# Four-layer graph attention stack: the third layer's PSUM banks emptied by one ScalarE copy with the relu, reciprocal and scaling done in SBUF

## Chip, cores and metric

One core of one Trainium2 chip runs the whole program. The metric is the device time of one execution in microseconds. A run before the change took 2668.16 us (median of 3 runs, 2663.21 to 2668.47).

## What is computed

16 graphs of 1024 nodes with 256 features pass through four attention layers, each with a layer norm and a relu ahead of it and a residual behind it. The first three layers have four heads of 64 features, the fourth has one head of 256. The third layer, which the change touches, is (cut to what matters; in this stack `adj` holds 0 and 1 only):

```python
h = relu(layernorm(x)); h = einsum('bnd,hde->bhne', h, W)
weight = leaky_relu(e_src[..., :, None] + e_dst[..., None, :], 0.01)
attention = softmax(where(adj == 0, -1e9, weight), axis=-1)
dst = einsum('bhij,bhje->bhie', attention, h) + bias
out = relu(dst) + h
out = (out - mean(out)) / sqrt(var(out) + 1e-6) * gamma + beta    # over each head's 64 features
x = x + out
```

## The kernel before, in words

**One head.** The nodes are cut in 8 blocks of 128. For a head, VectorE makes 8 tiles `p` of 128x1024: the numerators of the softmax from one block of nodes to all 1024. `cover` makes one in a single instruction out of a row `r` (128x1024, in PSUM), a factor `fac` for each node of the block and the mask. There are 12 buffers for `p` (`p0` to `p11`). TensorE then multiplies each tile with the block's values `vals`, which carry one more column, so that column 64 of the product is the softmax's denominator. `gather` does that for one half of the 1024 nodes: 8 matmuls, and 8 tiles add up in one PSUM bank `po` of 128 x 4 x 65. The two halves of a head are two groups with a bank each, the second some tiles behind the first. There are two such banks (`ps_o`, `bufs=2`), so a new group can start only when the group before the last one has been emptied.

**Emptying a bank.** `evacuate` runs once for each group. In the first two layers (`u.shared`) ScalarE copies the whole bank, 128x260, into an SBUF tile `att` (three buffers, `ATTS`). In the third layer the bias is already added to the values (`v_flat`), and the bank is emptied in this order: VectorE takes the reciprocal of the four denominators out of PSUM into `inv`; then ScalarE reads each of the four 128x64 blocks out of PSUM, scales it by its reciprocal, applies the relu and writes it to `att`. After both halves `finish` adds `h` on GpSimd (`att <- att,v`), takes statistics on VectorE (`st <- att`), normalizes on ScalarE (`att <- att,s`), and adds to `x_cur` on GpSimd.

**What else ScalarE does.** It copies the rows `r` from SBUF to PSUM (`spread_row`, 128x1024), each up to 3 tiles before the head that uses it; it turns the relu and copies of the projections out of PSUM (`hT`, `v`); it checks the masks (`seen`), scales the fourth layer's results (`y`).

**The order of the work.** The order on every engine is fixed when the program is built: a planner (`Plan`) keeps an estimated free time for each engine and steps through jobs, which are generators; each `yield` names the engine of the next step and when it may go. Of the steps that could start next on an engine, it takes the one that is due first. The wrappers `act`, `dve`, `pe`, `pool` and `sp` issue an instruction and book its estimated cost with `plan.spend`; a call through `nc.scalar` or `nc.vector` issues it without booking it. On the chip each engine runs its list in order and waits with semaphores. Since most instructions are recorded by the wrapper, the profile gives nearly all of them line 515; they are told apart by their tiles. The graphs and layers are interleaved by the table `ORDER`, so that the work of two or three layers of different graphs is in flight at a time.

The lines that the text needs: the banks `ps_o` (617), `cover` (1218), `gather` (1278), `evacuate` (1312), `finish` (1341).

Of the kernel before, what the change touches and what calls it, by code (L numbers as in the profile page):

```python
# [16 lines left out]
AF = mybir.ActivationFunctionType  # L17
# [519 lines left out]
def fast_path(  # L537
# [21 lines left out]
    nc = tc.nc  # L559
    ctx.enter_context(tc.manual_schedule())  # L560
    plan = Plan()
    pe, act, dve, pool, sp = (
        plan.engine(e, name)
        for e, name in (
            (nc.tensor, "PE"),
            (nc.scalar, "ACT"),
            (nc.vector, "DVE"),
            (nc.gpsimd, "POOL"),
            (nc.sync, "SP"),
        )  # L570
# [5 lines left out]
    QUAD = 4  # L576
# [701 lines left out]
    def gather():  # L1278

        u, i, h, j, p, slot, _ = covered.pop(reach()[1])  # L1280
        w = u.w
        if (u, i, h) not in groups:
            groups[u, i, h] = [sums_bank(w + 1), 0, len(opened)]
            opened.append(None)
        g = groups[u, i, h]
        po = g[0]
        at = h * (w + 2)
        for q in range(QUAD):


            for c in range(0, P, P // 2):
                pe.matmul(
                    po[c : c + P // 2, q, :],
                    p[:, q * P + c : q * P + c + P // 2],
                    u.vals[:, j, at : at + w + 1],
                    start=(g[1] == 0 and q == 0),
                    stop=(g[1] == NB - 1),
                    skip_group_check=True,
                )
        leave(slot)  # L1300
        g[1] += 1
        if g[1] == NB:
            u.gathered, u.last = u.gathered + 1, plan.now
            u.v_done = u.v_done or u.shared and u.gathered == 2 * H
            add(-(10**6), evacuate(u, i, h, po, g[2]), plan.now)
# [6 lines left out]
    def evacuate(u: "Unit", i: int, h: int, po, turn: int):  # L1312

        w = u.w
        q = slice(i * QUAD, (i + 1) * QUAD)
        yield "ACT" if u.shared else "DVE", lambda: finishing[0] < ATTS or (u, h) in taking
        if (u, h) not in taking:
            finishing[0] += 1
            taking[u, h] = [work.tile([P, NB, w + 1], F32, name="att", bufs=ATTS), 0]
        att = taking[u, h][0]  # L1320
        if u.shared:
            act.copy(att[:, q, :], po)
        else:
            inv = u.inv[:, h, q]
            dve.reciprocal(inv, po[:, :, w])
            yield "ACT", None
            for k in range(QUAD):
                act.activation(att[:, i * QUAD + k, :w], po[:, k, :w], AF.Relu, scale=inv[:, k : k + 1])
        opened[turn] = plan.now
        taking[u, h][1] += 1  # L1330
        if taking[u, h][1] == 2:

            by = -(10**6) if u.layer < 2 or at_tile[0] > len(tiles) - LAST else at_tile[0] + LATER
            add(by, finish(u, h, att[:, :, :w], att[:, :, w]), plan.now)
# [249 lines left out]
    def add(until, gen, ready, first=None):  # L1584
        jobs.append([until, ready, *(first or next(gen))[:2], gen])
# [103 lines left out]
```

## Time and profile before

| | |
|---|---|
| runs | 2663.21, 2668.16, 2668.47 us |
| profiled execution | 2667.53 us, span 2665.8 us, granted clock 0.997 |
| PE busy, weight loads (PEld) | 2578.2 us, 2207.9 us |
| VectorE (DVE) | 2342.0 us, 3723 instructions |
| ScalarE (ACT) | 1272.3 us, 3378 instructions |
| GpSimd (POOL) | 1890.4 us |
| DMA | 184.44 MB, mean 69 GB/s |

The span is the time from the first instruction to the last. A group's row in the profile names line, engine, operation, `out<-in` by tile, the shape and the number of instructions; behind the bar stand the busy time in us and the mean of one in ns, and behind the second bar the idle time of that engine just ahead of the group's instructions and what ended it. A row of the order of time gives start, length, engine, the group and, in brackets, the idle time before it and its releaser. An idle time "by issue" is one that no other instruction ended.

### The profile page before, as it was taken

The page shows a single profiled execution, that of the slowest core. Times are in us where ns is not written, and L with a number is a line of the kernel's source. Part 1 is how long each engine was busy: PE and PEld are TensorE (multiplying, and loading weights), DVE is VectorE, ACT ScalarE, POOL GpSimd, SP SyncE. Part 2 cuts the span into 40 slices and gives each one's busy share as a digit, 9 for nine tenths or more (in the row PEclk, how much of TensorE's full clock was granted, in tenths as well). Part 3 has the DMA queues.
Part 4 walks back from the last instruction along what each step waited for, and adds up shares of the span by engine and source line. Part 5 has one row for each costly group of instructions (what it writes and reads, how often), then busy time and mean ns, then how long its engine had stood idle before and what let it go on. Part 6 is the DMA issues. An engine that isn't in the chain of part 4 may idle for free. (4 is left out here: it accounts for less than half of the span.)

```text
span 2665.8 us, 132436 instructions
## 1 busy us (share of the span) xinstructions
PE 2578.2 (97%) x59354; PEld 2207.9 (83%) x59354; DVE 2342.0 (88%) x3723; ACT 1272.3 (48%) x3378; POOL 1890.4 (71%) x3375
## 2 busy tenths in 40 slices
PE   9999999999999999999999999999999999899998
PEld 7888887787988788889888788988778798888775
DVE  6799998897999797889998897999888699998984
ACT  4633563654346456533564644356364553443441
POOL 5556888765778877747887875688787565977761
PEclk9999999999999999999999999999999999999999
DMA  8533233443132253313314441323334441111100
GB/s 133 84 75 73 59 69 69 76 87 71 64 66 63 63 85 82 76 57 77 72 55 82 88 72 59 83 50 75 74 74 79 83 85 57 53 47 55 40 23 32
DMA packets 211122, 184.44 MB, mean 69 GB/s; under 512 B 150640, under 2 KB 184560, under 8 KB 210544
## 3 DMA queue, kind: packets, MB, share of 16 engines
q1 hardware_dynamic: 143088, 159.10, 20.7%
q0 software_dynamic: 67456, 16.78, 10.3%
q8 instruction: 467, 7.65, 1.2%
q14 instruction: 111, 0.91, 0.1%
HBM read 191.77 MB, written 34.39 MB: 85 GB/s over the span
## 5 line engine op out<-in xcount | busy, mean ns | idle before, releaser
L515 DVE SCALAR_TENSOR_TENSOR p<-r,fac,mask 128x1024 f32<-128x1024 f32 (+2 forms) x2032 | 2075.7, 1079 | 159.8 <-PE pp L515 80.8
L515 PE MATMUL po<-v,p 128*64 128x65 f32 x32992 | 1060.9, 224 | 36.4 <-issue 15.8
L515 PEld LDWEIGHTS po<-v,p 128*64 128x64 f32 x32992 | 1021.5, 138 | 87.9 <-issue 30.8
L515 PEld LDWEIGHTS po<-v_flat,p 128*64 128x64 f32 x16384 | 507.8, 138 | 56.8 <-issue 24.4
L515 PE MATMUL po<-v_flat,p 128*64 128x65 f32 x16384 | 525.0, 223 | 29.4 <-issue 14.7
L515 PE MATMUL pp<-wa,hT 128*64 128x264 f32 (+1 forms) x4032 | 474.2, 385 | 0.1
L515 PE MATMUL pp<-v_one,p 128*64 128x257 f32 x3584 | 403.6, 380 | 3.2 <-ACT y L515 2.9
L515 PEld LDWEIGHTS pp<-wa,hT 128*64 128x64 f32 x4032 | 278.4, 137 | 132.1 <-ACT v L515 0.4
L515 PEld LDWEIGHTS pp<-v_one,p 128*64 128x64 f32 x3584 | 248.6, 136 | 128.0 <-ACT y L515 4.6
L515 POOL TENSOR_SCALAR hn<-x_cur,rs 128x256 f32<-128x256 f32 x504 | 274.6, 558 | 33.3 <-PE pp L515 29.3
L515 POOL TENSOR_TENSOR att<-att,inv 128x512 f32<-128x512 f32 x128 | 133.7, 1045 | 221.2 <-DVE inv L515 207.7
L515 ACT COPY att<-po 128x260 f32<-128x260 f32 x256 | 96.2, 376 | 377.1 <-PE po L515 353.1
L515 ACT COPY v<-pp 128x264 f32<-128x264 f32 (+1 forms) x392 | 148.5, 379 | 215.0 <-PE pp L515 213.8
L515 POOL TENSOR_TENSOR x_cur<-att,x_cur 128x512 f32<-128x512 f32 x190 | 225.8, 1188 | 14.9
L515 ACT COPY r<-rows 128x1024 f32<-128x1024 f32 x190 | 194.0, 1021 | 21.8 <-DVE p L515 15.5
L515 ACT ACTIVATE att<-att,s 128x64 f32<-128x64 f32 x512 | 190.9, 439 | 23.3 <-POOL s L515 23.0
L515 ACT ACTIVATE hT<-pp 128x512 f32<-128x512 f32 x250 | 136.4, 598 | 128.1 <-PE pp L515 127.4
L515 ACT ACTIVATE att<-po,inv 128x64 f32<-128x64 f32 x512 | 118.7, 321 | 145.6 <-DVE inv L515 143.6
L515 POOL TENSOR_TENSOR y<-y,x_cur 128x256 f32<-128x256 f32 x116 | 84.3, 732 | 131.6 <-ACT y L515 112.1
L515 POOL TENSOR_TENSOR v<-v,fac 128x512 f32<-128x512 f32 x131 | 136.2, 1064 | 11.5 <-ACT fac L515 11.4
L515 DVE BATCH_NORM_STATS2 st<-x_cur 128x6 f32<-128x256 f32 x400 | 138.3, 411 | 3.3 <-DMA x_cur<-in_x_dram 2.9
L515 PE MATMUL pp<-ident,hn 128*128 128x128 f32 x1000 | 137.0, 280 | 0.2 <-DVE row L515 0.2
(124 smaller groups left out, 2150.0 us busy)
## 6 DMA issues: line engine op xcount, KB each, us to landing
rows<-line SPq DMA_DIRECT2D x190, 512.0 KB
out_dram<-y SPq DMA_DIRECT2D x128, 128.0 KB
x_cur<-in_x_dram SPq DMA_DIRECT2D x112, 128.0 KB
near<-in_adj_dram POOLq DMA_DIRECT2D x112, 128.0 KB, 4.3
rows_one<-line SPq DMA_DIRECT2D x13, 512.0 KB
x_cur<-in_x_dram SPq DMA_DIRECT2D x4, 512.0 KB
line<-row SPq DMA_DIRECT2D x96, 8.0 KB
block<-in_adj_dram POOLq DMA_DIRECT2D x4, 256.0 KB, 10.4
```

Of the source, the lines that this page charges most:

```text
L515: r = call(*a, **k)
```

## The change

In the third layer's branch of `evacuate` the bank is emptied by one ScalarE instruction, which applies the relu and copies all four blocks with their denominators (128x260) to `att`. VectorE takes the reciprocals from `att` in SBUF, and ScalarE scales the four 128x64 blocks in place in `att`. The denominators are positive, and so are the factors, so that relu and scaling may change places. The copy is not booked in the plan; the reciprocal and the scalings are booked with the costs that they had.

```diff
         if u.shared:
             act.copy(att[:, q, :], po)
         else:
             inv = u.inv[:, h, q]
-            dve.reciprocal(inv, po[:, :, w])
+            nc.scalar.activation(att[:, q, :], po, AF.Relu)
+            nc.vector.reciprocal(inv, att[:, q, w])
+            plan.spend("DVE", *plan.cost("DVE", "reciprocal", (inv,), {}))
             yield "ACT", None
             for k in range(QUAD):
-                act.activation(att[:, i * QUAD + k, :w], po[:, k, :w], AF.Relu, scale=inv[:, k : k + 1])
+                one, of = att[:, i * QUAD + k, :w], inv[:, k : k + 1]
+                nc.scalar.activation(one, one, AF.Copy, scale=of)
+                plan.spend("ACT", *plan.cost("ACT", "activation", (one, of), {}), [], [att.tensor.name])
```

## Prediction

> **What bounds the kernel now.** I read the page's first part, then the busy time of each engine by stretch, then the weight loads and the order of time inside one stretch, and last the groups by form. The page alone points at TensorE:
>
> ```profile
> PE 2578.2 (97%) x59354; PEld 2207.9 (83%) x59354; DVE 2342.0 (88%) x3723; ACT 1272.3 (48%) x3378; POOL 1890.4 (71%) x3375
> ```
>
> The table by stretch says otherwise for a part of the run. Its columns are the stretch, its length, then busy time and count for PE, PEld, DVE, ACT and POOL.
>
> ```profile
> 758.40:829.90 71.50, 67.42 (x1944) 62.19 (x1940) 71.33 (x109) 40.35 (x124) 60.45 (x106) 1.00 0.26 55
> 1246.30:1317.60 71.30, 66.99 (x1947) 62.02 (x1941) 71.26 (x108) 40.23 (x124) 61.27 (x108) 1.00 0.26 55
> 1731.70:1802.90 71.20, 66.59 (x1919) 61.36 (x1915) 71.20 (x110) 40.28 (x124) 61.31 (x108) 1.00 0.27 55
> 2261.50:2332.80 71.30, 63.91 (x1790) 59.41 (x1786) 71.03 (x122) 32.40 (x93) 63.70 (x111) 0.98 0.17 55
> 829.90:1246.30 416.40, 408.81 (x9151) 346.26 (x9151) 362.68 (x578) 201.60 (x524) 299.22 (x536) 1.00 0.34 74
> ```
>
> The run repeats every 488 us. In each period there is a stretch of 71 us in which VectorE is busy for 71.3 of 71.5 us; the same holds for 270 to 342 us (71.75 of 72.00). In the other 416 us VectorE has 54 us of idle time and TensorE is the bound. That PE reads 94% inside a stretch is its pipelining; the weight loads at the end of one stretch show who leads:
>
> ```profile
> 822.83 1.01 PEld L515 LDWEIGHTS po<-v,p 128*64 128x64 f32 x32 [0.18 <-DVE p L515]
> 824.02 1.01 PEld L515 LDWEIGHTS po<-v,p 128*64 128x64 f32 x32 [0.18 <-DVE p L515]
> 825.21 1.01 PEld L515 LDWEIGHTS po<-v,p 128*64 128x64 f32 x32 [0.18 <-DVE p L515]
> 826.40 1.01 PEld L515 LDWEIGHTS po<-v,p 128*64 128x64 f32 x32 [0.18 <-DVE p L515]
> ```
>
> Every tile is waited for: 1.19 us from tile to tile, VectorE's own pace, while 1.01 us of loading would do. So a microsecond put into VectorE there lengthens the run, and a microsecond taken from TensorE earlier in the stretch is only waited out later in it.
>
> [...] By the 97% the sum below would be rival A; by the weight loads (87% in the stretch, VectorE 99.8%) it is the forecast.
>
> **The change, part by part.** 16 graphs x 4 heads x 2 halves make 128 evacuations. The built programs hold the same instructions in the same order on PE, DVE, POOL and SP, so no DMA moves. Only ScalarE gets 128 more instructions, each where the planner chose the reciprocal. The rows:
>
> ```profile
> L515 ACT COPY att<-po 128x260 f32<-128x260 f32 x256 | 96.2, 376 | 377.1 <-PE po L515 353.1 <-POOL hn L515 11.3 <-POOL x_cur L515 9.9
> L515 ACT ACTIVATE att<-po,inv 128x64 f32<-128x64 f32 x512 | 118.7, 321 | 145.6 <-DVE inv L515 143.6 <-DVE wide L515 0.8
> L515 DVE RECIPROCAL inv<-po 128x4 f32<-128x4 f32 x128 | 22.5, 176 | 21.4 <-PE po L515 20.3
> L515 PE MATMUL po<-v_flat,p 128*64 128x65 f32 x16384 | 525.0, 223 | 29.4 <-issue 14.7 <-ACT att L515 10.8 <-DVE p L515 1.5
> ```
>
> 1. *The added copy.* The same shape without the relu takes 0.376 us; at 128x512 the relu (598 ns) is 12 ns over the copy (586 ns). So 0.38 us, and 128 x 0.38 = 49 us of ScalarE, which is idle for 52% of the span. Off the path by itself; its price is in whom it delays.
>
> 2. *The bank.* Before, it was held from the group's end through the reciprocal and four scalings (0.93 us): 1.2 us at least and 1.65 us in the middle one of the 128. Now about 0.43 us. TensorE waited 10.8 us for it. All of these waits but one (0.26 us) lie in or beside the five stretches, for instance:
>
> ```profile
> 768.10 0.33 DVE L515 RECIPROCAL inv<-po 128x4 f32<-128x4 f32 x2
> 768.37 1.75 ACT L515 ACTIVATE att<-po,inv 128x64 f32<-128x64 f32 x8 [6.40 <-DVE inv L515]
> 769.35 1.85 PE L515 MATMUL po<-v_flat,p 128*64 128x65 f32 x56 [1.15 <-ACT att L515]
> ```
>
> With the bank free earlier TensorE starts earlier and is then late for nothing but VectorE's tiles, as it already was by 771.9. Worth about 0 where VectorE leads; 10.8 us is the other end.
>
> 3. *The reciprocal's new wait.* It now stands behind the copy: group end + 0.05 + 0.38 + 0.03 us, or later if ScalarE is busy. Behind it on VectorE stand all later covers (1.19 us each), for which TensorE waits. The stretch at 758, from the records of each instruction (group ends are the last matmul's):
>
> | evacuation | group ends | VectorE came | new copy ends | wait added |
> |---|---|---|---|---|
> | 1 | 758.28 | 758.37 | 758.71 | 0.37 |
> | 2 | 760.15 | 760.83 | 760.97 | 0 |
> | 3, 4 | 767.73, 768.20 | 768.10, 768.24 | 768.16, 768.63 | 0.42 for both |
> | 5 | 781.80 | 782.44 | 782.23 | 0 |
> | 6 | 782.27 | 783.70 | 784.5 | 0.8 |
> | 7 | 794.30 | 794.63 | 795.1 | 0.45 |
> | 8 | 796.28 | 797.16 | 797.6 | 0.45 |
>
> Row 2 is covered by the shift of row 1. In row 6 the copy queues behind the four scalings of row 5, and these behind a row copy (1.02 us) that row 5's copy holds up. In rows 7 and 8 it queues behind work that ScalarE has already begun (a row copy until 794.78; scalings until 797.27). Sum 2.5 us. Read the same way, the stretches at 270, 1246, 1732 and 2261 give 2.2, 2.5, 2.1 and 1.6 us. Together 10.9 us, all on the path, since VectorE has no idle time left there to absorb it.
>
> 4. *The other 88 evacuations* (and their waits, 0 to 1.4 us each, some 39 us by the same reckoning) fall where tiles lie 0.7 to 20 us ahead of TensorE and VectorE still idles, mostly for TensorE. Covered: 0. Without that cover: 39 us.
>
> 5. *Scalings from SBUF.* No row shows one with a single scalar operand. Bounds: 0.23 us each as now, from PSUM; 0.345 us as the normalization's `att<-att,s` (SBUF, two scalar operands; eight in 2.76 us). I take the first, the nearer in operands; the other adds 0.45 us to four scalings, which reaches VectorE only in row 6: at most 2 us in all. The reciprocal's source: 176 ns from PSUM, 196 ns for 128x8 from SBUF: nothing. [...]
>
> 6. *What is held up behind the copy.* On ScalarE: four row copies (at 265, 752, 1241 and 1727 us) that now wait 4 to 6 us for a group's end; the cover that first reads such a row stands behind four other covers and two sets of statistics, 5 us and more after the new copy's end, so 0. The `hT` and `v` copies come at most 0.15 us late by the same reckoning: 0 to 1 us. The copy also takes its `att` buffer sooner than the scalings did, from POOL; the scalings never waited for POOL in the trace, so 0.
>
> 7. *The end.* The last graph's third layer feeds its fourth, and TensorE idles at 2587 (2.8 us) and 2607 us (1.8 us) for that chain. One evacuation is 0.4 us longer, two if both halves count: 0.8 us.
>
> Sum: 10.9 + 0.8 = about +12 us. The profiled execution took 2667.53 us (span 2665.8), by 0.6 us the median of the runs shown (2668.16). I forecast **2679 us**. Faster or slower by 0.2% is 5.3 us, about what can be told from no change.
>
> **Rivals.**
>
> A. *TensorE is the bound throughout* (page: 97%) and the bank waits come off: 2667.5 - 10.8 = 2657 us. It decides if VectorE's lead in the stretches is regained before the next one, that is if the waits in step 3 find idle time. Against it: 0.2 us of idle time in 71.5. Chance 0.12.
>
> B. *Hidden.* The gain of step 2 pays for step 3, or the copies find ScalarE earlier than I queue them (rows 6 to 8 fall away): 2664 to 2672, say 2669. For it: TensorE runs several us behind VectorE in the middle of each stretch. Chance 0.2.
>
> C. *More than queued.* Waits add up since each shifts the next group's end, and part of step 4's 39 us or the slower scalings reach the path: 2667.5 + 12 + a third of 39 + 2 = 2695 us. Against it: slack of 4 us and more at most of the 88. Chance 0.1.
>
> Forecast (2673.5 to 2688): 0.58. That the change does not do what it says is excluded by the built program.
>
> **Range.** 2663 to 2692: it leaves out most of A and the upper part of C. Faster 0.12, same 0.2, slower 0.68.
>
> **What would show it.** The wait "PE po<-v_flat <- ACT att" falls from 10.8 us to about 1; the 128x4 reciprocal's idle time rises from 21 us to 50 to 80, ended by "ACT att"; the five stretches grow from 71.5 to 73 to 74 us with VectorE's busy time unchanged, while the 416 us between them stay; ScalarE's busy time rises by about 49 us. The forecast is wrong if the stretches keep their length, if the part between them grows, or if VectorE has idle time in a stretch that is not before these reciprocals.

## The result, and the profile after

The changed kernel takes 2693.58 us (2688.12 to 2696.00, five runs) against 2668.47 us (2663.21 to 2671.81, five runs) before: a ratio of 1.009, 95% interval 1.0073 to 1.0108, +24 us (19 to 29). It is slower, as forecast, by twice as much: 2693.58 lies 1.6 us above the range. The profiled execution took 2688.12 us (span 2686.3), the fastest of its five, so that the two traces differ by 20.5 us where the medians differ by 25.

The page's first part of the changed kernel:

```profile
PE 2590.5 (96%) x59354; PEld 2212.1 (82%) x59354; DVE 2343.9 (87%) x3723; ACT 1330.4 (50%) x3506; POOL 1885.7 (70%) x3375
```

VectorE has the same 3723 instructions and the same work. ScalarE has 128 instructions and 58 us more: the copy takes 49 us and the scalings 17 us more than before (135.7 against 118.7), while its other groups have 7 us less in sum (the `v` copies 142.7 against 144.0, the relu to `hT` 135.1 against 136.4, the rest less each). The groups by form (behind the second bar: the engine's idle time ahead of them, and who ended it):

```profile
L515 PE MATMUL po<-v_flat,p 128*64 128x65 f32 x16384 | 524.8, 223 | 24.9 <-issue 15.4 <-DVE p L515 5.8 <-ACT att L1331 1.1
L515 PE MATMUL pp<-wa,hT 128*64 128x264 f32 x3040 | 360.1, 387 | 9.9 <-ACT hT L515 5.7 <-ACT v L515 2.0 <-DVE c L515 1.9
L1331 ACT ACTIVATE att<-att,inv 128x64 f32<-128x64 f32 x512 | 135.7, 338 | 31.3 <-DVE inv L1326 31.2
L515 PE MATMUL pp<-wa,hT 128*64 128x258 f32 x992 | 116.1, 381 | 3.7 <-ACT v_one L515 3.4
L1325 ACT ACTIVATE att<-po 128x260 f32<-128x260 f32 x128 | 48.7, 380 | 100.7 <-PE po L515 99.7
L1326 DVE RECIPROCAL inv<-att 128x4 f32<-128x4 f32 x128 | 22.4, 175 | 50.2 <-ACT att L1325 49.7
```

The copy takes 380 ns, as estimated. TensorE's wait for the bank is nearly gone (10.8 us before; now 1.1 us behind L1331 and 0.8 us behind L1325). The reciprocal's idle time is 50 us where it was 21, and the copy ends it. The two rows `pp<-wa,hT`, the projections, are new as waits. In the kernel before they were:

```profile
L515 PE MATMUL pp<-wa,hT 128*64 128x264 f32 x3040 | 358.4, 386 | 0.1
L515 PE MATMUL pp<-wa,hT 128*64 128x258 f32 x992 | 115.8, 380 | 0.0
```

From 0.1 and 0.0 us they rose to 9.9 and 3.7 us, for `hT`, `v` and `v_one`, which ScalarE makes, and 1.9 us of them for `c`, which VectorE makes.

Busy time by stretch, three of the five stretches and then the part between the second and third (columns as in the prediction; each stretch begins and ends at the same matmul as before):

```profile
761.81:837.84 76.03, 68.35 (x1944) 62.51 (x1940) 71.94 (x110) 44.65 (x133) 61.71 (x108) 1.00 0.27 59
1258.66:1332.98 74.32, 68.33 (x1946) 62.60 (x1940) 72.01 (x109) 44.63 (x133) 61.79 (x109) 1.00 0.28 60
1749.89:1823.03 73.14, 67.82 (x1918) 62.00 (x1914) 71.49 (x108) 43.82 (x132) 61.23 (x108) 1.00 0.29 62
837.84:1258.66 420.82, 410.52 (x9152) 347.57 (x9152) 362.22 (x577) 208.10 (x540) 297.85 (x535) 1.00 0.34 72
```

These three stretches grow from 71.2 to 71.5 us to 73 to 76 us while VectorE's busy time grows by 0.3 to 0.8 us: it now waits. But the part between them grows too, from 416.40 to 420.82 us, and that the forecast excluded. Part of this is given back elsewhere: TensorE's idle times by "issue" ahead of the matmuls into `po` add up to nearly the same over the run (30.5 us before, 30.2 us now) but lie differently, some 7 us more of them in the stretches and as many fewer outside.

**Where the time came from.** TensorE runs the same list in both kernels, so each matmul's start can be set beside its start before. The shift grows in two kinds of places: by 1.9 to 4.5 us in each of the five stretches, and by 2.4 us (the last: 1.0) in each of five regions right behind them, at 347 to 388, 834 to 876, 1322 to 1364, 1807 to 1850 and 2340 to 2385 us of before. These belong to the third layer of graphs 1, 4, 7, 10 and 13; the stretches belong to that of graphs 0, 3, 6, 9 and 12. Stretches and regions make 15.2 and 10.6 us. Elsewhere the shift goes up and down, mostly with the pauses by issue, and gives back 5.3 us in sum, which leaves the 20.5 us between the two traces.

### The profile page after: what moved, and what is told of

Its sections match the earlier page's. It is cut to its first block, busy times and chain, and to the rows that moved or that the text cites. A ratio compares the mean times of both kernels' runs of the same rounds, so it can differ in the third digit from the quotient of the medians.

```text
span 2686.3 us, 132594 instructions
## 1 busy us (share of the span) xinstructions
PE 2590.5 (96%) x59354; PEld 2212.1 (82%) x59354; DVE 2343.9 (87%) x3723; ACT 1330.4 (50%) x3506; POOL 1885.7 (70%) x3375
## 3 DMA queue, kind: packets, MB, share of 16 engines
q0 software_dynamic: 67456, 16.78, 10.1%
## 5 line engine op out<-in xcount | busy, mean ns | idle before, releaser
L515 ACT COPY r<-rows 128x1024 f32<-128x1024 f32 x190 | 193.5, 1018 | 16.7 <-DVE p L515 13.7
L515 ACT ACTIVATE hT<-pp 128x512 f32<-128x512 f32 x250 | 135.1, 591 | 125.5 <-PE pp L515 125.1
L1331 ACT ACTIVATE att<-att,inv 128x64 f32<-128x64 f32 x512 | 135.7, 338 | 31.3 <-DVE inv L1326 31.2
L515 POOL TENSOR_TENSOR v<-v,fac 128x512 f32<-128x512 f32 x131 | 136.0, 1060 | 12.4 <-ACT fac L515 12.4
```

The lines of the kernel that those rows point to most:

```text
L515: r = call(*a, **k)
L1331: nc.scalar.activation(one, one, AF.Copy, scale=of)
```

## The experiments

**Theory 1.** In the stretches, whatever makes VectorE wait lengthens the run; the change does that through the reciprocal's wait for the copy. In the five regions, ScalarE's longer chain stands ahead of the projections' copies, for which TensorE waits. **Theory 2.** ScalarE's longer queue is itself the price in the stretches too. **Theory 3.** The price follows ScalarE's time, evenly over all graphs.

All kernels but two keep the order of TensorE's list, so this table could be made for them: growth of the five stretches, VectorE's idle time in them by what ended it (in the kernel before it has 0.7 us in all), growth of the five regions, and the whole as ratio minus 1 with its interval, times the time before. All in us.

| kernel | stretches | idle, for the third layer's copy | idle, other | regions | whole |
|---|---|---|---|---|---|
| the change | 15.2 | 12.8 | 0.9 | 10.6 | +24 (19 to 29) |
| e1 graphs 0, 3, 6, ... | 17.1 | 15.2 | 0.9 | 0 | +11 (6 to 15) |
| e2 graphs 1, 4, 7, ... | 1.4 | 0 | 1.7 | 10.6 | +11 (6 to 15) |
| e3 graphs 2, 5, 8, ... | 2.2 | 0 | 2.5 | 0 | +1 (-2 to 4) |
| e4 reciprocal first | 11.2 | 0 | 10.1 | 7.4 | +16 (11 to 21) |
| e5 copy behind | 2.6 | 0 | 2.7 | 3.6 | +7 (4 to 10) |
| e6 denominators first | 8.6 | 7.9 | 0.9 | 5.3 | +18 (12 to 23) |
| e9 reciprocal from PSUM | 12.6 | 11.1 | 0.3 | 10.6 | +21 (17 to 25) |
| e10 scalings behind | 14.0 | 12.4 | 0.8 | 8.1 | +25 (21 to 30) |
| e11 GpSimd multiplies | 25.4 | 0 | 26.9 | 0.1 | +17 (12 to 21) |
| e12 GpSimd alone | 40.5 | 0 | 43.2 | 0 | +31 (26 to 35) |
| e13 reciprocal later | 11.1 | 2.2 | 8.1 | 13.0 | +29 (24 to 33) |
| e14 scalings at the finish | 27.1 | 22.8 | 3.2 | 7.7 | +66 (62 to 70) |
| e15 both | 10.4 | 1.1 | 9.1 | 7.9 | +49 (45 to 53) |

The third and fourth columns add up to the second within 2.8 us in every row: **a stretch grows by what VectorE idles in it, whatever it waits for.** This sum has to come out where VectorE's busy time stays the same, so it does not show the cause by itself. What the columns tell is that VectorE had next to no idle time to give before, and what ended the idle time in each kernel. The growth of stretches and regions does not add up to the whole, since TensorE's pauses by issue move in and out of them, and the traces are of single executions.

### One third of the graphs at a time (e1, e2, e3)

```diff
+            changed = u.g.b % 3 == 0          # e2: == 1, e3: == 2
+            if changed:
                 nc.scalar.activation(att[:, q, :], po, AF.Relu)
                 nc.vector.reciprocal(inv, att[:, q, w])
...
+            else:
+                dve.reciprocal(inv, po[:, :, w])
```

> The change made only for graphs 0, 3, 6, 9, 12 and 15; the rest empties its banks as before. The third layers of graphs 0, 3, 6, 9 and 12 lie in the five stretches in which VectorE has no idle time. Theory 1 (two costs: VectorE's wait for the copy in the five stretches, and ScalarE's longer chain ahead of the hT, v and v_one copies elsewhere): the whole first cost and none of the second, +11 to +14 us against before, and PE's waits for ACT hT and v_one stay as before. Theory 2 (all is VectorE's wait): +20 us or more. Theory 3 (ScalarE's added time as such, 49 us of it spread over 128 evacuations): 48 of 128, about +9 us, in proportion to the 25.

> The change made only for graphs 1, 4, 7, 10 and 13, whose evacuations fall where tiles lie 3 to 14 us ahead of TensorE. Theory 1: about +9 us (some 2.2 us for each of graphs 1, 4, 7 and 10, less for 13), with TensorE's waits for ACT hT, v_one and v as in the changed kernel (some 10 us together). Theory 2 and the prediction on record: 0, since VectorE's lead covers its waits. Theory 3: 40 of 128, about +8 us, but spread evenly over A, B and C.

> The change made only for graphs 2, 5, 8, 11 and 14, whose evacuations fall with tiles 0.7 to 20 us ahead. Theory 1: 0 to +4 us, one v or hT copy late here and there (a shift of 1 us stands in the changed kernel's trace at 949 us of before). Theory 2: 0. Theory 3: 40 of 128, about +8 us as in the runs of A and B.

Measured: 1.0041 (1.0024 to 1.0058), 1.0040 (1.0024 to 1.0055) and 1.0005 (0.9994 to 1.0016). The three add up to 0.0086, the whole change to 0.009. Theory 3 falls: the same work costs 11 us in each of two thirds of the graphs and about nothing in the last. What e1 expected of the projections was wrong in part: the 5 us of TensorE's wait for `hT` belong to the stretches and stay there, while `v_one` (3.4 us) and `c` (1.9 us) go with e2, and the 2.0 us for `v` with e3.

What happens in a region, the list of ScalarE in the kernel before (start, length, then the group; in brackets idle time and releaser):

```profile
846.73 0.92 ACT L515 ACTIVATE att<-po,inv 128x64 f32<-128x64 f32 x4
847.52 1.11 ACT L515 ACTIVATE hT<-pp 128x512 f32<-128x512 f32 x2
848.47 1.07 ACT L515 COPY r<-rows 128x1024 f32<-128x1024 f32 x1
849.42 0.98 ACT L515 ACTIVATE att<-po,inv 128x64 f32<-128x64 f32 x4
850.21 0.82 ACT L515 COPY v_one<-pp 128x258 f32<-128x258 f32 x2
```

and in the changed kernel:

```profile
854.66 0.38 ACT L1325 ACTIVATE att<-po 128x260 f32<-128x260 f32 x1
855.29 1.06 ACT L1331 ACTIVATE att<-att,inv 128x64 f32<-128x64 f32 x4 [0.25 <-DVE inv L1326]
856.26 1.06 ACT L515 ACTIVATE hT<-pp 128x512 f32<-128x512 f32 x2
857.21 1.01 ACT L515 COPY r<-rows 128x1024 f32<-128x1024 f32 x1
858.16 0.38 ACT L1325 ACTIVATE att<-po 128x260 f32<-128x260 f32 x1
858.78 1.07 ACT L1331 ACTIVATE att<-att,inv 128x64 f32<-128x64 f32 x4 [0.24 <-DVE inv L1326]
859.75 0.62 ACT L515 COPY v_one<-pp 128x258 f32<-128x258 f32 x2
```

From the first emptying's start to the `v_one` copy's it was 850.21 - 846.73 = 3.48 us and is 859.75 - 854.66 = 5.09 us: 0.8 us more for each of two emptyings, made of the copy (0.38 us), the turn to VectorE and back (0.25 us idle) and scalings that take 1.06 instead of 0.92 us (the second four 1.07 instead of 0.98). The projection behind it, TensorE's list of the changed kernel, had no such wait before:

```profile
860.15 1.96 PE L515 MATMUL pp<-wa,hT 128*64 128x258 f32 x16 [0.84 <-ACT v_one L515]
```

Of a region's 2.4 us, about 1.0 us comes at this wait and about 0.6 us, 18 us later, at one of 0.47 us for `c`; the rest is spread over smaller steps.

### ScalarE's time without the wait, and the wait almost without ScalarE's time (e4, e5, e6)

```diff
 # e4: reciprocal out of PSUM first; the copy waits for it
-            nc.scalar.activation(att[:, q, :], po, AF.Relu)
-            nc.vector.reciprocal(inv, att[:, q, w])
+            dve.reciprocal(inv, po[:, :, w])
...
+            nc.scalar.activation(att[:, q, :], po, AF.Relu, scale=inv[:, 0:1])
 # e5: the kernel before, and behind its scalings
+            nc.scalar.activation(att[:, q, :w], att[:, q, :w], AF.Relu)
 # e6: the kernel before, but
-            dve.reciprocal(inv, po[:, :, w])
+            nc.scalar.copy(inv, po[:, :, w])
+            nc.vector.reciprocal(inv, inv)
```

> VectorE takes the reciprocal out of PSUM as before; then ScalarE copies the bank and scales in SBUF, directly one after the other. The copy takes the first reciprocal as its scale, so that it has to wait for VectorE; the results are scaled once too often by it, which leaves part of the computation other than the reference's. VectorE waits for ScalarE nowhere, ScalarE has the same 128 copies and 512 scalings, and the bank is held until the copy's end. Theory 1: the first cost (11 to 14 us) goes, the second stays in part, since the copy and the longer scalings (0.38 + 0.14 us) stay ahead of the hT copies but the turn to VectorE and back (0.25 us) goes: +5 to +10 us. Theory 2: 0. Theory 3: +25 us.

> The kernel before, with one ScalarE instruction more in each of the 128 evacuations: behind the four scalings it applies the relu to their 128x256 results once more, in place (the result stays the same). VectorE waits for no copy, the bank comes free as before, the scalings read PSUM; the order of all other work is that of before. Theory 1 (in the stretches the reciprocal's wait costs, in graphs 1, 4, 7, 10, 13 ScalarE's longer chain ahead of the projections' hT and v copies): 0.38 + 0.03 us of the 0.76 us that the change added to an evacuation there, so half of the 2.4 us, +1.2 us in each of these graphs, 0 in the five stretches; +5 to +6 in all. Theory 2 (ScalarE's longer queue is itself a price in the stretches too, by row copies and evacuations that come late for VectorE and TensorE): also some +1 us in each stretch, +10 in all. Theory 3 (turn to VectorE and back is the whole price): 0 in both.

> The kernel before, but ScalarE first copies the four denominators alone (128x4) from PSUM to SBUF, VectorE takes the reciprocal there, and the four scalings read PSUM as before. The reciprocal waits for ScalarE as in the change, but there is no large copy, no scaling from SBUF, and the bank is held longer. Estimate for the small copy 0.2 us. Theory 1: the reciprocal's wait in the stretches goes from 2.5 us each to what 0.2 instead of 0.38 us and the queue leave of it, +1.5 to +2.5 each, and the chain in graphs 1, 4, 7, 10, 13 is 0.2 + 0.25 us longer in place of 0.76, +1.4 each: +13 to +17 in all, and VectorE's wait for the copy stays above 25 us. Theory 2 (ScalarE's time): in proportion to 0.2 of 0.5 us, +8.

Measured: 1.0061 (1.0042 to 1.0079), 1.0026 (1.0015 to 1.0037) and 1.0066 (1.0044 to 1.0087). e5 and e6 came within 1 us of what theory 1 had named: +7 for +5 to +6 and +18 for +13 to +17. For e5 that is partly luck: 0 was expected in the stretches and 1.2 us in each region, and 2.6 us in all and 0.4 to 0.8 us were found; its interval (4 to 10) does not exclude theory 2's +10 either. Together the two make about the change: 0.42 us of ScalarE's time behind the scalings costs 7 us, a wait for a copy of only 0.14 to 0.21 us costs 18 us, and the change, which has both, 24 us. The split is not a clean one, since e6 also puts the small copy and the turn to VectorE on ScalarE, and costs 5.3 us in the regions.

e4 cost more than expected (+16 for +5 to +10). VectorE waits for no copy of the third layer there, yet idles 10 us in the stretches, for things that come later from ScalarE: 4.4 us for copies of the first layers, 2.2 us for `v`, and 2.1 us for GpSimd's addition, ahead of the statistics `st`. So theory 2 has a part in it, but through VectorE again, and the reciprocal's wait is not the only way in which the added work costs time there. e4 is also not the change without the wait and nothing else: its copy, with a scale, takes 0.472 us, and TensorE waits 6.8 us for the bank. In e5, whose added instruction takes 0.42 us and stands ahead of the result as well, VectorE idles 2.7 us; what makes e4 so much dearer was not separated.

### The copy known to the planner, and GpSimd for the scaling (e7, e8)

```diff
 # e7: three steps of their own
+            act.activation(att[:, q, :], po, AF.Relu)
+            opened[turn] = plan.now
+            yield "DVE", None
+            dve.reciprocal(inv, att[:, q, w])
             yield "ACT", None
...
 # e8: the branch of the first two layers
+            act.activation(att[:, q, :], po, AF.Relu)
```

> The change, but the planner knows of the copy: it is a ScalarE step of its own that frees the bank, then the reciprocal is booked on VectorE, then the scalings on ScalarE. The order on all engines is planned anew. Theory 1: the reciprocals are put where the copy is done, so VectorE's wait for the copy falls from 50 us to under 10 and the stretches lose their 2.5 us each; ScalarE's longer chain stays, +5 to +10 against before. Rival (the price is the longer chain from group to result, wherever the reciprocal stands, or a new order is worse by itself): +15 to +30.

> The third layer's evacuation as that of the first two: one ScalarE copy with the relu, then one 128x8 reciprocal for each head on VectorE, and the multiplication on GpSimd (128x512, one for each head, 1.1 us); planned anew. ScalarE loses 119 us of scalings and gains 49 us, GpSimd gains some 70 us of 1886, VectorE loses 64 x (2 x 0.176 - 0.196) = 10 us, and the two evacuations of a head need one turn to VectorE and none back. Theory 1: both places of the price are gone and the projections' copies come 0.5 us earlier than before, -3 to -12 against before. Rival (GpSimd's chain behind the third layer, multiplication, additions, normalization, comes late for the fourth layer and for the next input): +5 to +20.

Measured: 1.0141 (1.0120 to 1.0163), +38 us, and 1.0384 (1.0361 to 1.0407), +103 us, both above all that was expected. In e7 both waits that theory 1 names are gone:

```profile
L515 PE MATMUL pp<-wa,hT 128*64 128x264 f32 x3040 | 365.9, 386 | 0.1
L515 PE MATMUL pp<-wa,hT 128*64 128x258 f32 x976 | 112.9, 380 | 0.0
L515 DVE RECIPROCAL inv<-att 128x4 f32<-128x4 f32 x128 | 20.4, 166 | 7.3 <-ACT att L515 7.3
L515 DVE RECIPROCAL inv<-pp 128x1 f32<-128x1 f32 x120 | 19.5, 163 | 72.2 <-PE pp L515 72.1
```

The reciprocal's wait fell from 50 to 7 us, the projections' waits to 0.1 us, and the kernel is slower still. Other waits came instead: VectorE's for the fourth layer's sums (last line) is 72 us, 27 us before; TensorE's for the tiles `p` is 38 us, 9 us before, and it waits 15 us for GpSimd's `v_flat` and `v`. A new plan moves everything, so e7 says nothing for or against the price of the two waits. It shows that this new order cost more than the 24 us in question. The same holds for e8, where GpSimd has 64 multiplications more (201.1 us of them, 133.7 before); which part of its 103 us is order and which is GpSimd was not separated. Both also ran at a lower granted clock (0.988 to 0.993 in e7, 0.985 to 0.987 in e8; 0.995 to 0.999 for the kernel before beside them), and what that adds was not separated either.

### The reciprocal back to PSUM, the scalings put off (e9, e10)

```diff
 # e9: the change, but
-            nc.vector.reciprocal(inv, att[:, q, w])
+            dve.reciprocal(inv, po[:, :, w])
 # e10: the change, but for graphs 1, 4, 7, 10, 13
-                nc.scalar.activation(one, one, AF.Copy, scale=of)
+                behind.append((one, of))      # issued behind the next act.copy(u.v[...])
```

> The change, but the reciprocal reads the denominators from PSUM, so that it waits for the group and no more for the copy; ScalarE copies and scales in SBUF as in the change; order and places as in the change. Theory 1 (VectorE's wait is the price in the stretches): they fall from +2.6 us each to what ScalarE's longer queue alone cost behind the scalings, +0.5 us; in graphs 1, 4, 7, 10, 13 the turn to VectorE (0.25 us) goes and copy and slower scalings stay, 0.5 of 0.8 us, +1.5 each: +8 to +11 in all. Rival (ScalarE's result is late by the same copy, and the stretches pay for that): stretches +1.3 each as with the reciprocal first, +13 to +16.

> The change, but in graphs 1, 4, 7, 10 and 13 the four scalings of an evacuation are put on ScalarE behind the next projection copy (hT, then v) in place of ahead of it; the copies out of PSUM, the reciprocals and the order on all other engines are those of the change. Theory 1: ScalarE then has 0.33 us of evacuation ahead of a projection's copies where the kernel before had 0.8 us, so TensorE's waits for hT and v_one (some 10 us of TensorE's shift) go, and the rest of the change stays: +10 to +14 against before in place of +23. Rival (those waits come from something else in these graphs): +20 and more.

Measured: 1.0079 (1.0065 to 1.0094) and 1.0095 (1.0079 to 1.0111), neither better than the change. e9 did not do what it was made for:

```profile
L515 DVE RECIPROCAL inv<-po 128x4 f32<-128x4 f32 x128 | 22.9, 179 | 50.5 <-ACT att L1325 49.9
```

Copy and reciprocal both only read the bank, but the second reader still waited for the first: 49.9 us, by the releasers of the profile, where it was 49.7 us in the change, and the price is the same within the interval. Where the reciprocal reads made no difference that can be seen (179 ns from PSUM, 175 from SBUF); a reciprocal free of the copy was not tried by this. In e10 the first projection copy came earlier, but the scalings of two emptyings then stood ahead of the next (lists of ScalarE, then of TensorE):

```profile
857.25 0.37 ACT L515 COPY v_one<-pp 128x258 f32<-128x258 f32 x1 [0.48 <-PE pp L515]
857.52 2.02 ACT L1317 ACTIVATE att<-att,inv 128x64 f32<-128x64 f32 x8
859.45 0.35 ACT L515 COPY v_one<-pp 128x258 f32<-128x258 f32 x1
```

```profile
859.85 1.09 PE L515 MATMUL pp<-wa,hT 128*64 128x258 f32 x8 [0.44 <-ACT v_one L515]
861.16 0.34 PE L515 MATMUL pp<-ident,wide 128*64 128x64 f32 x4 [0.22 <-ACT v_one L515]
```

The 0.84 us of wait became 0.44 and 0.22 us one copy later: the regions fell only from 10.6 to 8.1 us, far from the 0 that was expected.

### VectorE relieved, GpSimd loaded (e11, e12)

```diff
 # graphs 0, 3, 6, 9, 12: evacuate
+            nc.scalar.activation(att[:, q, :], po, AF.Relu)      # no reciprocal, no scaling
 # and finish
+                nc.vector.reciprocal(u.inv[:, h, :], total)      # e12: GpSimd, total to the power of -1
+                nc.gpsimd.tensor_mul(att, att, wide(u.inv[:, h, :]))
```

> The kernel before, with another evacuation in graphs 0, 3, 6, 9 and 12, those of the stretches: one ScalarE copy with the relu, no reciprocal and no scaling there; when the head is finished, VectorE takes one 128x8 reciprocal from SBUF and GpSimd multiplies (128x512); the other graphs and the order on TensorE and SP are as before. VectorE loses eight 128x4 reciprocals (8 x 0.2 us) in or beside each stretch and gains four of 0.2 us, later. Theory 1 (VectorE leads in the stretches): -0.8 to -1.4 us each, -3 to -7 in all. Rival (GpSimd's 4 x 1.2 us more for each of these graphs, or VectorE's wait for the second half's copy, comes late): 0 to +15.

> As the kernel with the multiplication on GpSimd in the graphs of the stretches, but GpSimd takes the reciprocal too, as a power of -1 (128x8), so that VectorE has none of it. Estimate from the power of -0.5 in the normalization: 1.65 us each. Theory 1: each stretch loses 8 x 0.2 us of VectorE, -1.4 each, -6 to -8 in all. Rival (GpSimd is busy for 61 of 71.5 us in a stretch and now has 4 x 2.9 us more): +5 to +25.

Measured: 1.0063 (1.0046 to 1.0080) and 1.0114 (1.0097 to 1.0132), +17 and +31 us: the rivals, by 2 and 6 us above the upper ends of their ranges. VectorE's waits in the third stretch (1258 to 1335 us) of e11:

```profile
DVE st L515 <- POOL att L515: 5.0, 4, 1.3
DVE inv L515 <- ACT att L515: 0.4, 1, 0.4
```

Four multiplications of 1.04 us each stand on GpSimd ahead of the addition whose result VectorE's statistics read; VectorE waits four times, up to 1.3 us, 5.0 us in all, and the stretch grows by 5.3 us. With the power on GpSimd too it waits 7.3 us there, and the stretch grows by 7.5 us. These two have no wait for the third layer's copy, and they show best that a stretch grows whoever makes VectorE wait. In the time of the whole run less arrives than in the stretches of one trace: 25.4 and +17 us in e11, 40.5 and +31 us in e12, 17.1 and +11 us in e1.

### The waits moved away (e13, e14, e15)

```diff
 # e13: graphs 0, 3, 6, ...: reciprocal issued one cover later, scalings one cover behind it
 # e14: graphs 1, 4, 7, ...: scalings issued when finish starts
 # e15: both
+            put_off.append([u, h, *{0: (1, 2), 1: (0, 99), 2: (0, 0)}[u.g.b % 3], steps])
```

> The change, but in the graphs of the stretches (0, 3, 6, 9, 12, 15) the reciprocal is issued on VectorE one cover (1.19 us) later, and the four scalings on ScalarE behind it, when one cover more has been issued. So VectorE does not wait for a copy that ended long before; ScalarE's work and all other order stay. Theory 1 (the reciprocal's wait on VectorE is the price in the stretches): they fall from +2.6 us each to +0.5 or less, the other graphs keep their +10: +10 to +14 in all, and VectorE's waits for the copy lose some 12 us or more. Rival (ScalarE's longer chain is the price there): stretches still +2 and more, +20 to +25.

> The change, but in graphs 1, 4, 7, 10 and 13 the four scalings are put on ScalarE only where the head is finished (some 30 tiles later), so that they do not stand ahead of the next projections' copies, and do not pile up ahead of a later v copy. Theory 1 (what stands on ScalarE ahead of the hT and v copies is the price in these graphs): their +2.4 us each go to 0 to +0.5, the stretches stay at +2.6: +11 to +15 in all. Rival (another cause in these graphs): +2 each again, +21 to +25.

> Both of these at once: the change with its copy where it is, the reciprocals of the stretches one cover later and the scalings of graphs 1, 4, 7, 10, 13 at the finish. Theory 1: +0 to +5; the bank is free early and nobody waits for the copy, so it ends level with the kernel before. Rival: +15 and more.

Measured: 1.0107 (1.0091 to 1.0122), 1.0246 (1.0232 to 1.0260) and 1.0184 (1.0170 to 1.0198), +29, +66 and +49 us: none is a repair, and all three lie above what theory 1 named. e13 took VectorE's wait for the copy away in the stretches (12.8 to 2.2 us), but 8.1 us of other waits came in its place. VectorE's waits in the third stretch of e13, 1257 to 1330 us:

```profile
DVE st L515 <- POOL att L515: 1.1, 1, 1.1
DVE inv L515 <- ACT att L515: 0.2, 1, 0.2
```

Here it waits for its own statistics' input, which comes later, as reciprocal and scalings were put later (half of the 8.1 us; the rest is first-layer copies and others). So with the reciprocal's wait taken away, 11.1 of the 15.2 us in the stretches stay, as they did in e4: the waits for the copy are where the change pays, but removing them alone does not give the time back. In e14 TensorE's wait behind the first emptyings is the one seen in e10, as `finish` begins between two `v_one` copies and all eight scalings again stand ahead of the second; beyond that GpSimd waits 92 us for the third layer's results (39 us in the change) and everything behind them is late. So the regions' price was not taken away by any kernel that kept the copy; that it comes from what stands ahead of the projections' copies rests on the two lists above and on the order e5 3.6, e6 5.3, e4 7.4, change 10.6 us, which follows what each puts there. Some of the 10.6 us also goes by VectorE: TensorE waits 1.9 us for `c`, which stands on VectorE behind a reciprocal. No kernel tried beats the one before.

## Why the prediction was wrong, point by point

- *What bounds the kernel* was right. VectorE leads in the stretches: it had 0.7 us of idle time in the five, and whatever made it wait there lengthened them (e1, e11, e12). That PE's 94% is pipelining shows in the row of its 16384 matmuls into `po`: 223 ns is the mean of one, but 525.0 us the busy time of all, 32 ns for each. TensorE's 97% would have made it a gain of 10.8 us (rival A). The period is less even than it was read: the stretches begin 488, 488, 485 and 530 us apart.
- *Step 1*, the copy: 0.38 us estimated, 0.380 measured.
- *Step 2*, the bank: its wait fell from 10.8 to 1.9 us (behind L1325 and L1331). Nothing of it is seen in the time, as said: VectorE's 0.7 us of idle time was all that the stretches could give, by the author's estimate. No run frees the bank and does nothing else.
- *Step 3*, the reciprocal's wait in the stretches: 2.2, 2.5, 2.5, 2.1 and 1.6 us forecast, 2.7, 4.1, 2.3, 1.6 and 2.0 us measured; 10.9 and 12.8 in sum, +11 us (6 to 15) by e1. Right in kind and near in size. The 4.1 us holds one pause of TensorE of 3.10 us by issue, just ahead of a group's end, which no reading of the trace before could place:

```profile
771.33 3.77 PE L515 MATMUL po<-v_flat,p 128*64 128x65 f32 x113 [3.10 <-issue]
774.39 0.18 DVE L1326 RECIPROCAL inv<-att 128x4 f32<-128x4 f32 x1 [2.41 <-ACT att L1325]
```

  VectorE was ready at 771.97 us and the group ended at 773.93 us, so that about 2.0 us of these 2.41 us are the pause and not the copy.
- *Step 6 is where it failed.* The `hT` and `v` copies were to "come at most 0.15 us late", for 0 to 1 us, and the sum took none of it. The change put 0.8 us more on ScalarE for each emptying ahead of them: 10.6 us in the five regions, +11 us (6 to 15) by e2. The 0.15 us came from asking when ScalarE could start its next instruction, and not how much longer its whole chain from group to projection copy becomes. Three terms were lost: the copy's own 0.38 us, counted "off the path by itself"; the turn to VectorE and back, 0.25 us in which ScalarE idles, as it has nothing else to issue in order; and 0.14 us of step 5.
- *Step 4*, the other 88 emptyings: "covered" holds for the third of the graphs that e3 changes (+1, -2 to 4). It does not hold for graphs 1, 4, 7, 10 and 13, though less by the reciprocal's wait, which it priced (about 0.6 us of a region's 2.4, through `c`), than by the projections' copies.
- *Step 5*: four scalings from SBUF take 1.06 us, 0.92 to 0.93 from PSUM. I took no difference; the other bound was +0.45 us. The rows show +0.14, between the two and nearer to the one that I took.
- *Step 7*, the end: 0.8 us said. In the trace the shift grows by 2.1 us from 2580 to 2590 us of before and has given 2.0 us of it back by 2610, so that nothing of it is left at the end.
- *Rival C* (2695) had the right time by luck: it expected a third of step 4's 39 us on VectorE, 13 us, and what came were the projections' copies. Its chance of 0.1 was too small since the sum held no term for ScalarE's chain.

## What to carry to other kernels

An instruction added to an engine that is half idle was not free here (ScalarE 48% busy, a copy of 0.38 us in each of 128 emptyings, +24 us for the change as a whole): look for what stands behind it on that engine's list, follow that to the engine that waits for it, and price the whole lengthened chain, turns to other engines included, not the next instruction's start. Where one engine leads without idle time, as VectorE does here in five stretches of 71 to 72 us (0.7 us idle in all), a wait put into it lengthened the stretch (15.2 us of growth with 13.7 us of waits), and taking that wait away gave back only a part, since other things were late by then (11.2 us of growth left in e4, 11.1 in e13). What emptying a PSUM bank early could bring here was at most what TensorE lost for the bank, 10.8 us of waits; they fell to 1.9 us, and nothing of it is seen in the time. That VectorE's lead is the reason is the author's estimate.

## What the runs showed of the hardware

Two readers of one PSUM bank on different engines ran one behind the other, though neither writes the bank (e9: 49.9 us of waits); the profile names the copy as the releaser, and whether the built program or the chip sets this order was not tried. TensorE's pauses by issue ahead of the matmuls into `po` have nearly the same sum in both kernels, 30.5 and 30.2 us (27.4 to 37.6 us in the experiments that keep TensorE's order), but not the same place: the kernel before has one of 1.17 us at 757 us and none of this size in the 12 us behind it; the changed kernel has one of 0.28 us there, and one of 3.10 us at 771 us. So in the changed kernel's trace this stretch is longer by about 2.0 us for that alone, and the effect of an edit is better read from the time of whole runs (e1, e2, e3), with the traces telling where it lies.
